# Two tiles for the squares of a layer normalisation, and one set of places for convolution inputs and feed-forward middle values

## The chip, the cores and the metric

The kernel runs as one program on 1 core of one Trainium2 chip. The metric is the device time of one execution in microseconds (us). Engine names: PE is TensorE's matmul, PEld its weight load, DVE is VectorE, ACT is ScalarE, POOL is GpSimd, SP is SyncE, which issues the DMAs of this kernel.

## The reference

The input is 4 images of 64 x 64 places with 96 channels. Each image goes through a chain of blocks:

```
x -> group norm -> 2-D selective scan (192 inner channels, 16 states, four scan directions) -> + x
  -> relu -> depthwise 3x3 convolution and pointwise product, batch norm            (layer1)
  -> + linear attention over the layer norm of the result                            (ln_a, attention)
  -> + feed-forward block over the layer norm of that, quantised to 8 bits           (q8, ffn2)
  -> + Fourier filter over the next layer norm                                       (ln_s, filter_*)
  -> + second quantised feed-forward block over a last layer norm                    (q8_3, ffn3)
```

The scan is h = exp(delta * A) * h + delta * u * B and y = sum over the states of h * C. A layer norm takes (x - mean) / sqrt(var + eps) over the 96 channels of a place. The feed-forward block rounds its operands to 8 bits and applies 96 -> 384 -> 96 channels with a relu between.

## The kernel before, in words

**The scans set the frame.** An image is held with channels on the partitions and 4096 places along them. The selective scan works on 192 phases (4 images, 2 orders of the places, 24 groups of 8 channels; 8 channels by 16 states fill 128 partitions). A phase has 4 chunks of 1024 places, gone through forwards and then backwards, so 8 steps. In a step ACT computes the decay exp(A * delta) into a PSUM tile `pa` (`decay`, L1495), DVE runs the scan (L1741 forwards, L1792 backwards) and adds the two directions (L1802), POOL multiplies by B and C (`times_b`, L1478, and `times_c`, L1482), PE sums over the states (`reduce`, L1509), ACT copies the sum (`result`, L1517), and SP loads and stores.

**Everything else is put beside the scans.** The other blocks are written as generators which yield a price per engine; after each step of a phase, `pieces` lets them advance as far as the step's credits go. This happens when the program is built: the order of instructions on each engine is fixed then, and every engine works through its own list in order. A side lane turns images for the second scan order and sums the scan's outputs; the main lane first prepares images 1 to 3 for their scans (`before_scans`), and then takes the rest of images 0, 1 and 2 (`rest`, with `deep` = 1), one after the other. The rest of image 3 comes after the last scan (`tail`, `deep` = 2). All beside the scans share 3 PSUM banks (`take` waits for a free one, and `give` hands it back).

**Around the change.** Each image has four layer norms (results `ln_a`, `q8`, `ln_s`, `q8_3`), each in two halves of 4 blocks of 512 places (`half_of`). For a block, PE subtracts the mean with one matmul into a PSUM bank (`p_mean`, L905). ACT copies it to SBUF (L894) and squares it into a tile `sq` (L897), both in `centred`, and then the bank is given back. PE averages the squares of the block into a part of the bank `p_var` (`variance`, L887). With `deep` = 1, the order inside a half is: mean matmul of block i, variance matmul of block i - 1, then the copy and square of block i. After four blocks, ACT, DVE and POOL form the reciprocal root (L926 to L937), PE spreads it (L957), and DVE scales (L948). With `deep` = 1 each half has one `sq` tile for its four squares; with `deep` = 2 it has four.

`layer1` reads its input in blocks of 8 rows plus a margin, into tiles `x` of 96 x 10 x 64 fp32 (2560 bytes in a partition) with two places (L820, loaded by L821), and 9 matmuls read each (L861). `feed_forward` holds the middle values of a block in `y16`, 128 x 3 x 512 fp16 (3072 bytes), two places as well (L1063, written by ACT at L785 and L794, read by POOL's cast to 8 bits at L1083). Both belong to the region `mid` of an image, in which layer1, three layer norms, the attention and the first feed-forward block are set up together. A pool gives each tag its own places; a tile that takes a place over waits for the work on the one that was there before.

Of the kernel before, what the change touches and what calls it, by code (L numbers as in the profile page):

```python
# [10 lines left out]
F32 = mybir.dt.float32  # L11
# [8 lines left out]
HW = 64  # L20
L = HW * HW
C = 96
# [4 lines left out]
BLK = 512  # L27
NBLK = L // BLK
RPB = BLK // HW
# [4 lines left out]
def conv_taps():  # L34

    return [(1, 1)] + [(y, x) for y in range(3) for x in range(3) if (y, x) != (1, 1)]


def tap_window(ky, kx, r0):

    dy, dx = ky - 1, kx - 1
    ra, rb = max(0, -dy - r0), min(RPB, HW - dy - r0)
    ca, cb = max(0, -dx), min(HW, HW - dx)
    return dy, dx, ra, rb, ca, cb
# [29 lines left out]
def layers(ctx: ExitStack, tc: tile.TileContext, a: dict, out):  # L74
# [48 lines left out]
    def steps_past(since, n):  # L123

        while ordered[0] and clock[0] < since + n:
            yield NEXT
# [53 lines left out]
    def rows_of(i):  # L180

        r0 = RPB * i
        return r0, max(r0 - 1, 0), min(r0 + RPB + 1, HW)
# [28 lines left out]
    def settle(held):  # L212


        while held:
            cost, f, args, since = held[0]
            if cost[1]:
                while ordered[0] and clock[0] == since and (clock[0] - 1) % 8 in (7, 0, 1):
                    yield NEXT
            yield cost  # L220
            held.pop(0)
            f(*args)

    def until(ready):
        while not ready():
            yield NEXT
# [549 lines left out]
    def blk(i):  # L776
        return slice(i * BLK, (i + 1) * BLK)
# [25 lines left out]
    def rest(b, take, deep, x1t=None, held=None):  # L803
# [9 lines left out]
        def layer1(wk):  # L813
            x3 = (x1[b] if x1t is None else x1t).rearrange("p (r w) -> p r w", w=HW)

            def load(i):
                r0, lo, hi = rows_of(i)
                if x1t is not None:
                    return x3[:, lo:hi, :], clock[0]
                x = wk.tile([C, RPB + 2, HW], F32, tag="x", name="x", bufs=2)  # L820
                nc.sync.dma_start(x[:, : hi - lo, :], x3[:, lo:hi, :])  # L821
                return x, clock[0]

            def arrived(i):
                return done.get(("x1", b), 0) >= min(i + 2, NBLK)

            yield from until(lambda: arrived(0))
            nxt = load(0)
            yield NEXT
            held = []  # L830

            def finish(i, p, give):
                nc.scalar.activation(
                    t[:, blk(i)], p, AF.Identity, scale=l1s[:, 0:1], bias=l1s[:, 1:2]
                )
                give()
                ready["t1"] = i + 1

            for i in range(NBLK):
                r0, lo, hi = rows_of(i)  # L840
                if nxt is None:
                    yield NEXT
                    yield from settle(held)
                    yield from until(lambda: arrived(i))
                    nxt = load(i)
                    yield NEXT
                (x, since), nxt = nxt, None
                if clock[0] < since + LANDING:
                    yield NEXT
                    yield from settle(held)  # L850
                    yield from steps_past(since, LANDING)
                p, give = yield from take("p_l1", C, held=held)
                p3 = p.rearrange("p (r w) -> p r w", w=HW)
                for k, (ky, kx) in enumerate(conv_taps()):
                    if k % 3 == 0:
                        yield (2.4, 0, 0, 0, 0 if k else 1)
                        if nxt is None and i + 1 < NBLK and arrived(i + 1):
                            nxt = load(i + 1)
                    dy, dx, ra, rb, ca_, cb_ = tap_window(ky, kx, r0)
                    at = r0 + dy - lo  # L860
                    nc.tensor.matmul(  # L861
                        p3[:, ra:rb, ca_:cb_], lhsT=taps[:, ky * 3 + kx, :],
                        rhs=x[:, at + ra : at + rb, ca_ + dx : cb_ + dx],
                        start=(k == 0), stop=(k == 8),
                    )
                    if k == 2:
                        yield from settle(held)
                held.append(((0, 0.68, 0, 0), finish, (i, p, give), clock[0]))
            yield NEXT
            yield from settle(held)  # L870

        def layernorm(wk, hold, dst, source, result, previous=None):
# [3 lines left out]
            def half_of(h):  # L876
# [6 lines left out]
                def variance():  # L883

                    i, sq = squares.pop(0)
                    at = 32 * (i - half[0])
                    nc.tensor.matmul(pv[at : at + 32, :], lhsT=mean_w, rhs=sq, start=True, stop=True)  # L887

                def centred(i, pm, give):
                    if squares and deep == 1:  # L890
                        variance()
                    sq = wk.tile([C, BLK], F32, tag=f"sq{h}", name="sq", bufs=1 if deep == 1 else 4)
                    if ordered[0]:
                        nc.scalar.copy(hold[:, blk(i)], pm)  # L894
                    else:
                        nc.vector.tensor_copy(hold[:, blk(i)], pm)
                    nc.scalar.activation(sq, pm, AF.Square)  # L897
                    give()
                    squares.append((i, sq))

                for i in half:
                    yield from until(lambda: count(source) > i)
                    pm, give = yield from take("p_mean", C, held=held)
                    yield (0.9, 0, 0, 0)
                    nc.tensor.matmul(pm, lhsT=centre, rhs=t[:, blk(i)], start=True, stop=True)  # L905
                    if squares and deep == 1:
                        yield (0.9, 0, 0, 0)
                        variance()
                    yield from settle(held)
                    held.append(((0, 1.25, 0, 0), centred, (i, pm, give), clock[0]))  # L910
# [415 lines left out]
        wk = normal.sbuf(f"ln{b}")  # L1326
# [8 lines left out]
        wk = mid.sbuf(f"mid{b}")  # L1335
# [24 lines left out]
        wk = last.sbuf(f"last{b}")  # L1360
# [287 lines left out]
    wk = weights.sbuf("weights", side="right")  # L1648
# [45 lines left out]
    wk = head.sbuf("pre0")  # L1694
# [14 lines left out]
    with tc.manual_schedule():  # L1709
        ordered[0] = True  # L1710
        pas = [decay(0, 0, True), None, None, None]
        for n in range(N + 1):
            h = n // NG
# [224 lines left out]
```

## Time and profile before

| | before |
|---|---|
| median of 3 runs | 5845.36 us (5842.83 to 5846.34) |
| profiled execution | 5842.19 us, span from first to last instruction 5840.4 us |
| busy: PE, DVE, ACT, POOL | 4230.1, 4797.6, 3044.6, 4416.6 us |
| mean granted TensorE clock | 0.775 of full speed |
| squares L897 in the scan part (images 0 to 2) | 96, median 592 ns, from 2029.1 to 5383.0 us |
| squares L897 in the tail (image 3) | 32 |
| ACT idle before the 96 squares | 75.2 us until p_var (43 times), 6.4 us until py (4 times) |
| a scan of 1024 places, L1741 | 2347 ns |
| a decay, L1495 | 1117 ns |

The busy time is the time in which an engine executes. The idle time listed with an instruction is the engine's time without work just before it; the name with it is the instruction that gave the last signal it waited for. An engine that is not the one on which the others wait in the end can idle at no cost. The first 520 us prepare image 0, from there to about 5440 us the scans run, and the last 400 us are the tail.

### The profile page before, as it was taken

Reading aid. Unit: us, or ns where it says so; the run is one execution under the profiler, and the core shown is the slowest. Engines: PE = TensorE matmul, PEld = TensorE weight load, DVE = VectorE, ACT = ScalarE, POOL = GpSimd, SP = SyncE. Lnnn points to the kernel's source line nnn. Section 1 sums busy time; section 2 is a strip of 40 time slices with the busy share of each in tenths; the row PEclk is TensorE's granted clock in tenths of the full one; section 3 lists DMA queues with packets and bytes.
Section 4 is the critical chain, followed back from the end, with each engine's and each line's share of the span. In section 5 each row is a group of like instructions: output and inputs, shape, how many; then the busy total and the mean of one; then the engine's idle time right before and its main releaser. Section 6 shows DMA issues by size and latency. Waiting matters only on the chain. (4 is left out here: it accounts for less than half of the span.)

```text
span 5840.4 us, 64640 instructions
## 1 busy us (share of the span) xinstructions
PE 4230.1 (72%) x19658; PEld 1612.3 (28%) x19658; DVE 4797.6 (82%) x3478; ACT 3044.6 (52%) x4205; POOL 4416.6 (76%) x2151
## 2 busy tenths in 40 slices
PE   8978888878973776664566776667678667667888
PEld 3322222222210221241331121245222114323345
DVE  2058898888899898998799999999999999979364
ACT  4667766766563346545454446444444554434233
POOL 1268888888889788888778989888898898867200
PEclk9979888888876776676777876668678767777888
DMA  3258878876698888788988867679887578886013
GB/s 105 80 163 233 234 215 225 242 221 195 187 253 237 222 216 223 206 243 237 246 240 224 228 185 211 194 212 249 230 235 206 164 210 235 245 230 191 22 39 104
DMA packets 469673, 1173.30 MB, mean 201 GB/s; under 512 B 90720, under 2 KB 155852, under 8 KB 469196
## 3 DMA queue, kind: packets, MB, share of 16 engines
q1 hardware_dynamic: 469324, 1169.17, 73.1%
q8 instruction: 156, 2.56, 0.2%
q14 instruction: 193, 1.58, 0.1%
HBM read 1012.05 MB, written 156.76 MB: 200 GB/s over the span
## 5 line engine op out<-in xcount | busy, mean ns | idle before, releaser
L1482 POOL TENSOR_TENSOR S<-S,rep 128x1024 f32<-128x1024 f32 x768 | 1807.6, 2356 | 541.5 <-DVE S L1802 485.4
L1495 ACT ACTIVATE pa<-dl,nega 128x1024 f32<-128x1024 f32 x1152 | 1285.3, 1117 | 1441.8 <-DVE S L1802 1076.0
L1478 POOL TENSOR_TENSOR B<-B,rep 128x1024 f32<-128x1024 f32 x768 | 1798.6, 2357 | 128.6 <-DMA B<-du_s 76.7
L1741 DVE TENSOR_TENSOR_SCAN S<-pa,S,B 128x1024 f32<-128x1024 f32 x576 | 1352.1, 2347 | 316.2 <-ACT pa L1495 128.6
L1509 PE MATMUL py<-S,red 128*32 128x512 f32 x3072 | 905.5, 845 | 739.9 <-POOL S L1482 491.4
L1792 DVE TENSOR_TENSOR_SCAN pa<-pa,edge,B 128x1024 f32<-128x1024 f32 x438 | 1029.7, 2351 | 46.3 <-ACT pa L1495 46.2
L1802 DVE TENSOR_TENSOR S<-S,pa 128x1024 f32<-128x1024 f32 x630 | 763.3, 1212 | 1.9
L1741 DVE TENSOR_TENSOR_SCAN S<-pa,B 128x1024 f32<-128x1024 f32 x192 | 436.4, 2273 | 189.5 <-ACT pa L1495 179.3
L390 PE MATMUL p_conv<-low,conv_w 128*96 128x512 f32 x1152 | 569.2, 647 | 8.7 <-ACT u L402 5.4
L1509 PEld LDWEIGHTS py<-S,red 128*32 128x32 f32 x3072 | 110.0, 125 | 1227.5 <-POOL S L1482 694.0
L1792 DVE TENSOR_TENSOR_SCAN pa<-pa,B 128x1024 f32<-128x1024 f32 x192 | 440.8, 2296 | 5.4
L154 ACT COPY side<-side 96x256 f32<-96x256 f32 (+1 forms) x448 | 278.9, 629 | 177.9 <-DMA deltaT_s<-side 74.5
L390 PE MATMUL p_conv<-high,conv_w 128*96 128x512 f32 (+1 forms) x768 | 356.6, 602 | 0.0
L1792 DVE TENSOR_TENSOR_SCAN dl<-pa,edge,B 128x1024 f32<-128x1024 f32 x138 | 323.1, 2341 | 16.3 <-ACT pa L1495 16.3
L1487 POOL TENSOR_TENSOR dl<-dl,rep 128x1024 f32<-128x1024 f32 x138 | 325.7, 2360 | 0.1
L1083 POOL CAST h<-y 128x1536 fp8e5<-128x1536 f16 x64 | 95.6, 1493 | 303.9 <-ACT y L794 286.3
L390 PEld LDWEIGHTS p_conv<-low,conv_w 128*96 128x96 f32 x1152 | 198.4, 179 | 390.8 <-issue 364.0
L905 PE MATMUL p_mean<-t,centre 96*96 96x512 f32 x256 | 174.8, 795 | 97.6 <-ACT sq L897 45.0
L1509 PE MATMUL py<-dl,red 128*32 128x512 f32 x552 | 219.2, 715 | 22.4 <-POOL dl L1487 22.3
L555 PE MATMUL p_y<-side,ident 96*96 96x512 f32 x336 | 207.1, 764 | 37.0 <-DVE q L948 11.6
L1517 ACT COPY ys<-py 128x512 f32<-128x512 f32 x384 | 221.9, 578 | 19.6 <-PE py L1509 18.2
L861 PE MATMUL p_l<-x,taps 96*96 96x504 f32 (+3 forms) x432 | 205.7, 629 | 16.4 <-DMA x<-x 12.5
(224 smaller groups left out, 5741.0 us busy)
## 6 DMA issues: line engine op xcount, KB each, us to landing
B<-du_s SPq DMA_DIRECT2D x768, 256.0 KB
dl<-delta_s SPq DMA_DIRECT2D x768, 256.0 KB
B<-duT_s SPq DMA_DIRECT2D x768, 256.0 KB
dl<-deltaT_s SPq DMA_DIRECT2D x768, 256.0 KB
z_s<-z SPq DMA_DIRECT2D x48, 512.0 KB
zl<-z_s SPq DMA_DIRECT2D x64, 384.0 KB
side<-y_s SPq DMA_DIRECT2D x120, 192.0 KB
rep<-bc_s SPq DMA_DIRECT2D x64, 256.0 KB
```

Source lines behind the costliest of these rows:

```text
L154: nc.scalar.copy(o.rearrange("p (w h) -> p w h", h=HW), t[:n, :].rearrange("p (h w) -> p w h", w=HW)[:, q * w : (q + 1) * w, :],)
L390: nc.tensor.matmul(p, lhsT=conv_w[: src.shape[0], k, oc * C : (oc + 1) * C], rhs=src[:, ky : ky + RPB, kx : kx + HW], start=(k == 0), stop ...
L555: nc.tensor.matmul(p, lhsT=ident[:C, :C], rhs=x, start=(j == 0), stop=(j == 2))
L1478: nc.gpsimd.tensor_tensor(Bs[n, q], Bs[n, q], reps[n // NG, 0, q], ALU.mult)
L1482: nc.gpsimd.tensor_tensor(Ss[n, q], Ss[n, q], reps[n // NG, 1, q], ALU.mult)
L1487: nc.gpsimd.tensor_tensor(dls[n, 0], dls[n, 0], reps[n // NG, 1, 0], ALU.mult)
L1495: nc.scalar.activation(pa, dls[n, q], AF.Exp, scale=nega[:, g : g + 1])
L1509: nc.tensor.matmul(py[32 * j : 32 * j + 32, :], lhsT=red, rhs=x[:, k * BLK : (k + 1) * BLK], start=(i == 0), stop=(i == len(terms) - 1),)
L1517: nc.scalar.copy(ys, pys.pop((n, half)))
L1741: nc.vector.tensor_tensor_scan(s, pas[q], Bs[n, q], Ss[n, q - 1][:, CH - 1 : CH] if q else 0.0, ALU.mult, ALU.add,)
L1792: nc.vector.tensor_tensor_scan(to[:, ::-1], pas[q][:, ::-1], Bs[n, q][:, ::-1], edge if k else 0.0, ALU.mult, ALU.add,)
L1802: nc.vector.tensor_tensor(Ss[n, q], Ss[n, q], to, ALU.add)
```

## The change

The convolution's input tile takes the tag `y16`, so that it shares the two places of the feed-forward block's middle values. The tile of the squares gets `2 * deep` places in each half: two instead of one beside the scans, four as before in the tail. In bytes of a partition of the region, 2 x 2560 go and 2 x 2048 come. An empty line moves the lines from 820 on by one in the changed kernel.

```diff
                 r0, lo, hi = rows_of(i)
                 if x1t is not None:
                     return x3[:, lo:hi, :], clock[0]
-                x = wk.tile([C, RPB + 2, HW], F32, tag="x", name="x", bufs=2)
+
+                x = wk.tile([C, RPB + 2, HW], F32, tag="y16", name="x", bufs=2)
                 nc.sync.dma_start(x[:, : hi - lo, :], x3[:, lo:hi, :])
                 return x, clock[0]
...
                 def centred(i, pm, give):
                     if squares and deep == 1:
                         variance()
-                    sq = wk.tile([C, BLK], F32, tag=f"sq{h}", name="sq", bufs=1 if deep == 1 else 4)
+                    sq = wk.tile([C, BLK], F32, tag=f"sq{h}", name="sq", bufs=2 * deep)
                     if ordered[0]:
                         nc.scalar.copy(hold[:, blk(i)], pm)
                     else:
                         nc.vector.tensor_copy(hold[:, blk(i)], pm)
                     nc.scalar.activation(sq, pm, AF.Square)
                     give()
                     squares.append((i, sq))
```

## The prediction

> **What bounds the kernel now.** The page first: busy time of each engine, then the costliest groups. Columns of a group: line, engine, operation, tiles and shapes, count | busy us, mean ns | idle of the engine just before it, and what ended it.
>
> ```profile
> PE 4230.1 (72%) x19658; PEld 1612.3 (28%) x19658; DVE 4797.6 (82%) x3478; ACT 3044.6 (52%) x4205; POOL 4416.6 (76%) x2151
> ...
> L1741 DVE TENSOR_TENSOR_SCAN S<-pa,S,B 128x1024 f32<-128x1024 f32 x576 | 1352.1, 2347 | 316.2 <-ACT pa L1495 128.6
> ...
> L1792 DVE TENSOR_TENSOR_SCAN pa<-pa,edge,B 128x1024 f32<-128x1024 f32 x438 | 1029.7, 2351 | 46.3 <-ACT pa L1495 46.2
> ```
>
> DVE is the busiest engine, and a scan waits most often for its decay tile, the exponential that ACT writes at L1495. The normalisation squares of images 0 to 2 lie between 2029 and 5383 us, so I asked for the stretch from 2000 to 5400 us (busy us and count of PE, PEld, DVE, ACT, POOL; granted PE clock; DMA share; GB/s):
>
> ```profile
> 2000.00:5400.00 3400.00, 2296.55 (x12618) 931.00 (x12618) 3100.90 (x2134) 1665.10 (x2269) 2862.38 (x1308) 0.73 0.81 220
> ```
>
> DVE is 91% busy there and idle for 299 us; POOL is next with 84%. So the time of this stretch is DVE's work plus its holes, and the wait that ends last in a hole decides. A faster ACT is worth only what it closes of these holes. Next, the line of the square, over the first 5500 us (who ended ACT's idle time before it, and who waited for it):
>
> ```profile
> L897 ACT ACTIVATE sq<-p_mean x96: 582/592/608, 2029.1 to 5383.0; 96x512 f32<-96x512 f32 x96
> ...
>   PE p_var L887: 75.2, 43
>   PE py L1509: 6.4, 4
> ...
>   PE p_mean L905: 45.0, 27
> ```
>
> ACT stands 81.6 us before 47 of the 96 squares, nearly all until PE has read the square before it. The timeline shows what that does (start, duration, engine, line, tiles, idle before and its releaser):
>
> ```profile
> 2029.71 2.02 PE L905 MATMUL p_mean<-t,centre 96*96 96x512 f32 x2 [2.09 <-ACT sq L897]
> ...
> 2031.66 1.91 PE L887 MATMUL p_var<-sq,mean_w 96*32 96x512 f32 x2
> 2031.77 0.58 ACT L894 COPY ln<-p_mean 96x512 f32<-96x512 f32 x1 [0.85 <-PE p_mean L905]
> ...
> 2033.67 0.59 ACT L897 ACTIVATE sq<-p_mean 96x512 f32<-96x512 f32 x1 [1.32 <-PE p_var L887]
> 2034.16 0.57 ACT L1517 COPY ys<-py 128x512 f32<-128x512 f32 x1
> ...
> 2034.63 1.12 ACT L1495 ACTIVATE pa<-dl,nega 128x1024 f32<-128x1024 f32 x1
> ...
> 2035.84 2.35 DVE L1741 TENSOR_TENSOR_SCAN S<-pa,S,B 128x1024 f32<-128x1024 f32 x1 [1.06 <-ACT pa L1495]
> ```
>
> The square holds ACT for 1.32 us after the copy, until the variance matmul of the previous square ends; a copy and the decay queue behind it, and the scan behind the decay starts 1.06 us late. PE's next mean matmul also waits for this square, because the square frees its PSUM bank.
>
> **What the skill says.** The Trainium skill, "Perfetto Trace Analysis", section "Per-engine timelines": an ACT instruction waits in its queue until all its semaphores are satisfied, and ACT and DVE are strict FIFO. The rows above agree: copy and decay run back to back once the square has gone. The same page, "Optimization Strategy", says to look for gaps on the most-contended engine and for the semaphore behind them, and that repeating gaps can mean too few buffers. The trace agrees for the square: its 47 holes average 1.74 us. No page prices this wait; all durations below are from the trace.
>
> **The change, part by part.** Order: the compiled instructions of PE, DVE, ACT, POOL and SP stand in the same order in both kernels, and nothing is added, removed or moved, no DMA either. Only waits differ.
>
> Part 1, convolution inputs in the feed-forward block's places: 24 loads at L821 keep two places and take turns as before. Each image's first use of a place by a middle value (L785) comes after all convolutions of that image, since it needs the second normalisation, which needs the whole attention. Cost nothing: those readers ended tens of us earlier. The tiles of this region lie elsewhere, which gives three ACT evacuations (L785, at 2486.43, 3764.67 and 4840.78) a later POOL instruction to wait for; in the trace it ends at 2440.13, 3718.45 and 4793.64, 46 us or more before it is needed. If that cover went, three waits would be at stake, some us each. The part alone: 0 us.
>
> Part 2, two squares a half: in each half's four squares (24 halves, 96 squares) the second loses its wait for PE, the third and fourth wait for a variance matmul one square older, on PE before the present mean matmul. In the sample that older matmul had ended 2 us or more before. The tail (image 3) had four tiles and keeps four, so its 32 squares do not change.
>
> What it is worth is not 81.6 us, since ACT is idle 51% of the stretch (1665 of 3400 busy). I went through the 47 waits, and took for each the DVE hole that the delayed decay causes, never more than the square's own wait. Starts of the scans and us: 2035.84 1.06; 2039.96 1.32; 2136.7 0.44; 2140.3 0.45; 2234.68 1.21; 2431.62 2.43; 3031 0.17; 3426.66 1.25; 3430.79 1.32; 3710.26 1.26; 4168.33 1.61; 4443.66 0.32; 4598.44 1.98; 4786.08 3.16; 5361 0.35. Sum 18.3. Behind the other waits the scans start without a hole that the decay causes.
>
> A second way goes over PE: the late square holds the PSUM bank, the attention product comes late, and DVE waits at L1037 with a scan queued behind. Waits of DVE between 3480 and 3512 us (total us, times, longest):
>
> ```profile
> DVE t L1037 <- PE p_att L1047: 4.7, 3, 2.3
> ```
>
> These three follow square waits of 3.01 and 2.50 us; with 0.28 and 1.47 us at 2212.42 and 2216.83, it is 6.45 us. At 4442.65 DVE waits 2.24 us for the rsqrt behind a square that itself waited 8.28 us (I take 1.8), and at 4595.77 1.06 us for p_rstd. Sum of this way 9.3. Both together: 27.6 us.
>
> What is late next: a scan that starts earlier meets its other feeders. After 2035.84 to 2039.96 the scan at 2062.48 starts only 0.09 us after a decay that waited 2.49 us for its DMA (issued at 2053.72 to 2054.89, behind other transfers on SP), so the 2.4 us won there can go again. With DMA busy 81% and POOL 84% of the stretch I keep three quarters: 21 us, and bounds of 0 (all given back) and 40 (half of the 81.6 reaches the end, because the halves also shorten PE's 45.0 us of waits at L905).
>
> Sum: profiled execution 5842.19 (span 5840.4, 1.8 around it) - 21 = 5821; the median of the three runs is 5845.36, 3.2 above the profiled one, so 5824.
>
> **Rivals.**
> A, the gain is given back: POOL and the transfers take the place of ACT as what ends the holes. For it: the scan at 2062.48, POOL at 84%, DMA at 81%. Against: of the DVE waits in the stretch 117 us end on the decay, while those that end on POOL or on the loads of B and dl are some 25 us together. It would leave about a quarter, 6 us: 5839.
> B, the gain is larger: PE's mean and variance chain runs without standing, everything beside the scans comes earlier, half of the 81.6 us counts: 5805. Against: ACT waits for DVE far longer (1076.0 us at L1495 behind L1802) than for PE here, so most of its time is free.
> C, slower: the same PE work in less time gets a lower clock. The clock is 0.73 in the stretch, against 0.81 between 560 and 1990 us[...]. A fall of 0.01 lengthens 2297 us of PE work by 31 us; DVE's waits that name PE are 59 of its 299 us of holes, so a fifth of that, 6 us, would reach the path. It decides against the change from a fall of 0.035 on; at 0.06 the time is 5845 + 36 - 21 = 5860. Against: nothing is added to PE, and 21 us of 3400 is 0.6% more load.
> D, no effect because the wait that went is not the last one: the copy before the square already waits for the mean matmul, 41.9 us in 23 waits. Against: in the rows above the square stands 1.32 us after the copy's end.
>
> **How the numbers follow.** Main case (half to all of 27.6 kept, 5818 to 5832) 0.62; A 0.19; B 0.08; C 0.07; D 0.04. About 0.2%, 12 us, is what a measurement tells from no change, so below 5833.7 counts as faster: the main case, B and a little of A (0.02), 0.72. A's rest and D are the same, 0.21. C is slower, 0.07. The range leaves out part of B and most of C: 5809 to 5845.
>
> **What would show it.** Right: at L897 the idle time until p_var falls from 75.2 us over the first 5500 us to below 25; DVE's waits for the decay between 2000 and 5400 us fall from 117 to about 100; DVE's share rises with the same busy time; everything before 2030 us and after 5440 us lasts as long as before. Wrong on giving back: the same fall at L897, but more waits of the scans for POOL or for loads. Wrong on the clock: less than 0.72 granted between 2000 and 5400 us. Wrong on part 1: any wait of L821 or L785 for POOL that was not there.

## The result and the profile after

| | before | changed |
|---|---|---|
| median | 5845.85 us (8 runs, 5840.30 to 5861.85) | 5826.24 us (8 runs, 5821.20 to 5830.70) |
| ratio | | 0.9965, 95% interval 0.9955 to 0.9975 |
| profiled execution, span | 5842.19, 5840.4 us | 5826.23, 5824.5 us |

The kernel became 19.6 us faster; the forecast was 5824 us with a range of 5809 to 5845. Measured once more beside other kernels, the ratio was 0.9951 (0.9934 to 0.9968). The page of the changed kernel, the lines that answer to those shown of before (lines from 820 on are one higher):

```profile
PE 4233.9 (73%) x19658; PEld 1615.2 (28%) x19658; DVE 4797.7 (82%) x3478; ACT 3044.1 (52%) x4205; POOL 4417.2 (76%) x2151
...
L1742 DVE TENSOR_TENSOR_SCAN S<-pa,S,B 128x1024 f32<-128x1024 f32 x576 | 1352.3, 2348 | 304.8 <-ACT pa L1496 108.5
...
L1793 DVE TENSOR_TENSOR_SCAN pa<-pa,edge,B 128x1024 f32<-128x1024 f32 x438 | 1029.8, 2351 | 46.8 <-ACT pa L1496 46.6
```

No engine works less: the busy times are those of before within 4 us. What went is idle time. Ahead of the first group of scans it fell by 11.4 us, from 316.2 to 304.8: the part that ended on the decay fell by 20.1 (128.6 to 108.5), and other waits of the same group grew by 8.7. The stretch from 2000 to 5400 us, and the line of the square over the first 5500 us (two of its 98 rows are the tail's):

```profile
2000.00:5400.00 3400.00, 2309.34 (x12644) 937.96 (x12642) 3114.54 (x2146) 1669.78 (x2275) 2874.97 (x1315) 0.73 0.82 221
```

```profile
L898 ACT ACTIVATE sq<-p_mean x98: 581/595/616, 2034.3 to 5500.0; 96x512 f32<-96x512 f32 x98
...
  PE p_var L888: 7.2, 8
...
  PE py L1510: 1.0, 1
...
  PE p_mean L906: 43.2, 19
```

The square's wait until PE has read the square before it fell from 75.2 to 7.2 us; with the waits until py, 47 holes of 81.6 us became 9 of 8.2. DVE does 13.6 us more of its unchanged work in the same 3400 us. The granted clock is 0.73 as before. The last line shows what hardly changed: PE's mean matmul still stands 43.2 us for a square (45.0 before), because the square gives its PSUM bank back; the experiments on the bank come to that.

The timeline of the changed kernel at the place that the prediction showed (start, duration, engine, line, tiles, idle before and its releaser):

```profile
2034.89 1.10 PE L906 MATMUL p_mean<-t,centre 96*96 96x512 f32 x2 [2.09 <-ACT sq L898]
...
2035.92 1.04 PE L888 MATMUL p_var<-sq,mean_w 96*32 96x512 f32 x2
2036.04 0.57 ACT L895 COPY ln<-p_mean 96x512 f32<-96x512 f32 x1
2036.52 0.59 ACT L898 ACTIVATE sq<-p_mean 96x512 f32<-96x512 f32 x1
2037.00 0.58 ACT L1518 COPY ys<-py 128x512 f32<-128x512 f32 x1
...
2037.46 1.13 ACT L1496 ACTIVATE pa<-dl,nega 128x1024 f32<-128x1024 f32 x1
...
2040.15 2.35 DVE L1742 TENSOR_TENSOR_SCAN S<-pa,S,B 128x1024 f32<-128x1024 f32 x1 [0.19 <-DMA yT_s<-ys]
```

The square now follows its copy at once, while PE is still at the variance matmul of the square before it; copy and decay follow. The scan behind this decay, which stood 1.06 us before, stands 0.19 us, and for a transfer. The order of the instructions is unchanged. One thing differs that the tiles do not explain: the mean matmul takes 1.10 us here and took 2.02 us before. That comes back below.

### The profile page after: what moved, and what is told of

It is laid out like the page before. It is cut to its first block, busy times and chain, and to the rows that moved or that the text cites. A ratio compares the mean times of both kernels' runs of the same rounds, so it can differ in the third digit from the quotient of the medians.

```text
span 5824.5 us, 64622 instructions
## 1 busy us (share of the span) xinstructions
PE 4233.9 (73%) x19658; PEld 1615.2 (28%) x19658; DVE 4797.7 (82%) x3478; ACT 3044.1 (52%) x4205; POOL 4417.2 (76%) x2151
## 5 line engine op out<-in xcount | busy, mean ns | idle before, releaser
L1742 DVE TENSOR_TENSOR_SCAN S<-pa,S,B 128x1024 f32<-128x1024 f32 x576 | 1352.3, 2348 | 304.8 <-ACT pa L1496 108.5
L1793 DVE TENSOR_TENSOR_SCAN dl<-pa,edge,B 128x1024 f32<-128x1024 f32 x138 | 323.1, 2341 | 15.5 <-ACT pa L1496 15.2
L906 PE MATMUL p_mean<-t,centre 96*96 96x512 f32 x256 | 175.7, 800 | 97.8 <-ACT sq L898 43.2
L862 PE MATMUL p_l<-x,taps 96*96 96x504 f32 (+3 forms) x432 | 200.9, 616 | 15.0 <-DMA x<-x 13.6
```

Source lines behind the costliest of these rows:

```text
L1742: nc.vector.tensor_tensor_scan(s, pas[q], Bs[n, q], Ss[n, q - 1][:, CH - 1 : CH] if q else 0.0, ALU.mult, ALU.add,)
L1793: nc.vector.tensor_tensor_scan(to[:, ::-1], pas[q][:, ::-1], Bs[n, q][:, ::-1], edge if k else 0.0, ALU.mult, ALU.add,)
```

## The experiments

All ratios are to the kernel before, measured on the same chip in the same row of runs.

**Each part alone.** Part 1: only the first edit.

```diff
-                x = wk.tile([C, RPB + 2, HW], F32, tag="x", name="x", bufs=2)
+                x = wk.tile([C, RPB + 2, HW], F32, tag="y16", name="x", bufs=2)
```

> Part 1 alone: the convolution inputs share the places of the feed-forward block's middle values, and each half keeps its one tile for squares. The forecast's own theory (the waits of the squares carry the gain): 0 us, a ratio of 1.000 within 0.0015, and ACT's idle time before the 96 squares until p_var stays at 75 us (65 to 85). Rival (the shared places, or where the tiles then lie, carry part of the gain): a ratio of 0.9985 or less, with waits of ACT, POOL or SP that become shorter at L821, L785 or L1083.

Measured: 0.9997 (0.9985 to 1.0009), and 75.9 us of waits for p_var before the squares. By itself the sharing is not told apart from nothing. It is meant for room: the second tile of each half adds 2 x 2048 bytes of a partition, and the sharing frees 2 x 2560. No run shows whether the tiles would fit without it.

Part 2 alone, in a form that needs no room:

```diff
-                    sq = wk.tile([C, BLK], F32, tag=f"sq{h}", name="sq", bufs=1 if deep == 1 else 4)
+                    sq = wk.tile([C, BLK], F32, tag="sq" if deep == 1 else f"sq{h}", name="sq", bufs=2 * deep)
```

> Part 2 alone, in another way: the two halves of a normalisation take turns on the two tiles for squares that they had one each of, so that a half has two, no byte is added, and the convolution inputs keep their own places. The squares theory: as the changed kernel, a ratio of 0.9965 (0.995 to 0.998), idle before the squares until p_var below 15 us. Rival (the sharing carries part): clearly less than the changed kernel, 0.998 or more.

Measured: 0.9947 (0.9926 to 0.9968) with 9.6 us left of the wait for p_var. The ratio lies just below the expected 0.995 to 0.998, so there is more gain than expected. Its interval covers the changed kernel's 0.9965, but both ran once more in one row:

> The changed kernel once more, beside the next three on the same chip: ratio to the kernel before 0.9965 (0.9955 to 0.9975). It gives the measure for the others of this row.

> The halves that take turns on two tiles, a second time, since the first measurement (0.9947, 0.9926 to 0.9968, of four executions) overlaps with the changed kernel's but lies lower. The squares theory: no difference to the changed kernel, 0.9965 within 0.001. Rival (the sharing of places costs some 10 us in the changed kernel, which the sharing alone did not show): 0.9947 again, and 0.0015 or more below the changed kernel of this row.

Measured: the changed kernel 0.9951 (0.9934 to 0.9968), the halves that take turns 0.9944 (0.9925 to 0.9963). The changed kernel's ratio lies a little below its expected range this time, so its gain is 20 to 24 us by the medians of the two rows. The two kernels of this row differ by 0.0007, less than the 0.0015 that the rival asked for and less than either interval. The squares make the gain, with or without the shared places; that the sharing costs a few us stays possible within these intervals.

**Is it the square's wait, or the time of ACT's pair?** One tile, PE's order changed:

```diff
+                    if squares and deep == 1:
+                        yield (0.9, 0, 0, 0)
+                        variance()
                     yield (0.9, 0, 0, 0)
                     nc.tensor.matmul(pm, lhsT=centre, rhs=t[:, blk(i)], start=True, stop=True)
-                    if squares and deep == 1:
-                        yield (0.9, 0, 0, 0)
-                        variance()
```

> One tile for squares as before, but PE does the variance matmul of the previous square ahead of the mean matmul of this block instead of after it, so that the square finds its tile free when the mean is there; nothing else is moved. Theory that the time of ACT's pair (copy and square) counts, whoever it waits for: the idle time before L897 until p_var falls below 10 us, but the mean matmul comes one variance matmul (1 to 2 us) later, the copy's wait for p_mean grows by 30 us or more, and most of the gain is lost: ratio 0.999 to 1.002. Rival (the square's wait as such is what costs, whatever takes it away): 0.9965 like the changed kernel.

Measured: 1.0009 (0.9999 to 1.0018). ACT's idle time before the copy (first fence) and before the square (second), first 5500 us:

```profile
  PE p_mean L908: 71.7, 39
```

```profile
  PE p_var L887: 57.5, 29
```

The square's wait did not fall below 10 us as expected, but only from 81.6 to 57.5: the last square of a half, whose predecessor's variance matmul stands outside the edited loop, still waits, 36.9 us of the 57.5 (31.7 before). The copy's wait rose from 41.9 to 71.7 us, as expected. So 24 us less wait before the square bought nothing: the copy ahead of it waited 30 us more. This fits the first theory, that the sum before the pair counts: 123.5 us before, 129.2 here, and 57.1 in the changed kernel, where no matmul is put later. The rival, 0.9965, is out.

**The bank.** One tile, the bank given back after the copy:

```diff
                         nc.scalar.copy(hold[:, blk(i)], pm)
+                        give()
+                        nc.scalar.activation(sq, hold[:, blk(i)], AF.Square)
                     else:
                         nc.vector.tensor_copy(hold[:, blk(i)], pm)
-                    nc.scalar.activation(sq, pm, AF.Square)
-                    give()
+                        nc.scalar.activation(sq, pm, AF.Square)
+                        give()
```

> One tile for squares as before, but the square reads the copy in SBUF instead of the PSUM bank, and the bank is given back after the copy, so that PE no longer waits for a late square to get a bank; ACT still waits for p_var before the square. If the second way (late bank, late attention product, 9.3 us in the forecast's sum) works through the bank: 7 us faster, ratio 0.9988 (0.998 to 0.9995), and DVE's waits for p_att at L1037 between 3480 and 3512 us fall from 4.7 to under 2.5 us. If the bank is not what counts: 1.000, with PE's wait for p_var's own square unchanged. In both cases the scans' holes behind the decay stay, since ACT's wait stays.

Measured: 0.9984 (0.9976 to 0.9993). That is as expected of a bank that counts, and 1.000 lies outside the interval: giving the bank back early gains with one tile too. The square itself became longer, 630 ns from SBUF against 592 from PSUM, and its wait shorter, 64.4 us with the part until py:

```profile
  PE p_var L887: 60.0, 36
```

The copy's wait for the mean fell as well, from 41.9 to 32.7 us. So the early bank also shortens the queue before copy and square, and the run doesn't separate the two ways of the forecast. The waits for p_att between 3480 and 3512 us were gone in this trace, but that is no evidence, as the part on the clock shows. The same edit on top of the changed kernel:

> The changed kernel, and the square reads the copy in SBUF, so that the bank goes back after the copy, some 0.5 us before the square's end in each of 96 blocks. In the changed kernel PE still stands 43 us at L906 for a square. If PE's wait for the bank still has a part on the path: 3 to 6 us below the changed kernel, 0.9955 to 0.9960, PE's waits at L906 for the square gone and for the copy about 35 us instead. If two tiles have taken all there was on this way: same as the changed kernel within 0.0005.

Measured: 0.9943 (0.9923 to 0.9964), against 0.9951 (0.9934 to 0.9968) of the changed kernel in the row. PE's waits for the square were gone and 33.5 us until the copy stood in their place, as expected; but the 3 us between the medians are inside the intervals, so what that is worth stays open.

**Is there more to be had?** Four tiles in one set (`tag="sq"`, `bufs=4` beside the scans), alone and with the bank's edit:

> The changed kernel with its four tiles for squares as one set for both halves, so that a half has four and no square waits for PE; no byte more. The changed kernel's rest of 8 us of waits at L898 goes to 0. The squares theory: of 8 us at most a third was on the path, so 0 to 3 us below the changed kernel: 0.9960 to 0.9966. Rival B of the forecast (more than the holes counted there is to be had from the chain of mean and variance matmuls): 0.9950 or less.

> Four tiles in one set for both halves, and the bank given back after the copy: both rests of the changed kernel taken away. If what is left of the squares' waits (8 us) and of PE's waits for the bank (43 us) is off the path: as the changed kernel, 0.9945 to 0.9965. If their small parts add: 0.9935 or less.

Measured: 0.9948 (0.9931 to 0.9965) and 0.9949 (0.9937 to 0.9961). No square waits for PE in either. Four tiles alone fall below the 0.9950 set for rival B, but the changed kernel itself measured 0.9951 beside them, so this border tells nothing. Neither version is told apart from the changed kernel (the second ran in another row, without it), and none is shown to beat it. Rival B's 40 us would be a ratio of 0.9932. That is outside both intervals of the changed kernel, though inside some of the wider ones of its relatives.

**Do the places add up?** Two tiles, shared by both halves, only in some normalisations (the other squares keep one tile a half; the second kernel has "q8" and "q8_3" instead). The edit is to the changed kernel, without its old line:

```diff
+                    twice = deep == 1 and result in ("ln_a", "ln_s")
+                    sq = wk.tile(
+                        [C, BLK], F32, tag="sqd" if twice else f"sq{h}", name="sq",
+                        bufs=2 if twice else 1 if deep == 1 else 4,
+                    )
```

> Two tiles for squares only in the normalisations ahead of the attention and of the Fourier filter (results ln_a and ln_s); the two ahead of the feed-forward blocks (q8 and q8_3) keep one. By the forecast's list these sites hold 14.8 of its 27.6 us; two of them (2.4 us, at 2036 and 2040 us) were holes of one execution's low clock, so 12.4, of which three quarters reach the end: 9 us, ratio 0.9984 (0.9975 to 0.9993). Idle before the squares until p_var falls to about half. Rival (one stretch gives all of it, or nothing adds up): below 0.997, or 1.000.

> The complement: two tiles only in the normalisations ahead of the feed-forward blocks (q8 and q8_3). The forecast's list holds 12.8 us there, 6.5 of them through the attention product; three quarters are 10 us: ratio 0.9983 (0.9975 to 0.9993), and together with the other half the 20 to 28 us of the changed kernel. DVE's waits for p_att at L1037 between 3470 and 3520 us go from 4.7 to below 2.5 us here and stay near 4.7 us in the other half. Rival as there.

Measured: 0.9966 (0.9952 to 0.9979) for ln_a and ln_s, 0.9981 (0.9971 to 0.9991) for q8 and q8_3. The second is as expected. The first is 20 us and not 9: its interval overlaps the expected one, but the ratio misses it and lies below the 0.997 set for the rival that one stretch gives all. That rival fails all the same, since the second kernel gains too, with 1.000 outside its interval. The two gains add up to 0.53%, which agrees with the 0.35% and 0.49% of the whole within the intervals. The waits before the squares were 53.3 and 35.5 us, so the kernel with more waits left had the larger gain by the medians; the intervals overlap. The sites in the traces, below, tell the two apart better.

**The clock.** The attention product was to show the second way, by DVE's waits for p_att. With two tiles only in ln_a and ln_s they were to stay near 4.7 us, and the trace has none there; in the kernel with two tiles and the early bank they are back, between 3480 and 3520 us:

```profile
DVE t L1040 <- PE p_att L1050: 4.1, 3, 1.9
```

What tells these executions apart is the clock granted to PE. First the kernel with two tiles and the early bank at that place, then the kernel before, then the changed kernel (busy us and count of PE, PEld, DVE, ACT, POOL; clock; DMA share; GB/s):

```profile
3494.00:3504.00 10.00, 10.00 (x15) 1.84 (x14) 6.14 (x5) 3.92 (x6) 8.62 (x4) 0.55 0.85 211
```

```profile
3494.00:3507.00 13.00, 11.18 (x14) 1.93 (x15) 9.11 (x7) 6.52 (x9) 13.00 (x6) 0.50 0.74 215
```

```profile
3490.00:3503.00 13.00, 11.70 (x36) 2.50 (x36) 12.97 (x12) 8.71 (x12) 11.76 (x7) 1.00 0.92 226
```

At half clock DVE has its holes there; at full clock it has none. One tile or two makes no difference to that. (Only the doubled matmuls, below, have 1.8 us there at full clock.) Part 1 alone, with one tile, also met half clock there (0.50 from 3502 to 3514 us) and has the holes (first). The kernel with two tiles only in ln_a and ln_s, so with one at this place, met full clock and has none (second):

```profile
DVE t L1037 <- PE p_att L1047: 4.8, 3, 2.3
```

```profile
3490.00:3503.00 13.00, 9.17 (x27) 1.78 (x26) 12.96 (x10) 8.70 (x12) 11.76 (x6) 1.00 0.85 231
```

The same holds for the place of the timeline, before (first) and with part 1 alone (second), both with one tile:

```profile
2030.00:2034.00 4.00, 3.57 (x4) 0.29 (x3) 4.00 (x3) 1.83 (x3) 4.00 (x2) 0.50 1.00 204
```

```profile
2036.00:2040.00 4.00, 3.26 (x11) 0.64 (x10) 3.89 (x3) 3.33 (x7) 4.00 (x3) 1.00 0.86 212
```

With part 1 alone the square there waits 0.45 us instead of 1.32, and the scan behind it has no hole that the decay causes. So those two sites of the forecast's list (2.4 us) and the three at p_att (4.7 us) were holes of the clock that the execution happened to have there, and their closing in the changed kernel's trace is not shown to be the tiles' doing.

**More of the wait.** One tile, each variance matmul done twice beside the scans:

```diff
-                    nc.tensor.matmul(pv[at : at + 32, :], lhsT=mean_w, rhs=sq, start=True, stop=True)
+                    for _ in range(2 if ordered[0] else 1):
+                        nc.tensor.matmul(pv[at : at + 32, :], lhsT=mean_w, rhs=sq, start=True, stop=True)
```

> One tile for squares as before, and PE does each of the 96 variance matmuls beside the scans twice in a row (the second writes the same sums again), so that the wait of the next square gets longer by one such matmul, 1.0 us at the full PE clock and some 2 us at half of it. ACT's idle time before the 96 squares should grow from 82 us by 60 to 90 us. The changed kernel took 74 us of it away and became about 20 to 24 us shorter, so 0.28 to 0.33 of a us of this wait reaches the end: 17 to 30 us longer, ratio 1.003 to 1.005. Rival (PE's chain itself is the bound, the wait only shows it): all 96 doubled matmuls, some 130 us, appear in good part, ratio 1.010 or more. Rival (only single sites at low clock matter): no change, 1.000 to 1.001.

Measured: 1.0089 (1.0072 to 1.0105), 52 us by the ratio and 50 between the medians, more than the theory. The first rival's border, 1.010, lies inside the interval. Before the squares stand 130.5 us:

```profile
  PE p_var L888: 125.0, 50
  PE py L1510: 5.5, 4
```

That is 49 us more, less than the expected 60 to 90, and the end moved by about as much. It is not the price of the wait alone: the added matmuls also delay what PE does next. DVE's waits for p_rstd grew from 34.6 us (2000 to 5400 us) to 54.8 (2000 to 5450 us in this longer kernel), those for the decay from 117.3 to 140.4. The expectation was missed. The variance matmuls alone are busy 99 us more, and about half of that reaches the end; the run gives no coefficient for the tile.

**The forecast's sites in all traces.** Ten entries of the forecast's list, from 2234.68 to 5361 us (without 3031, and with the 1.8 us of the second way at 4443), come to 16.7 us. For each I took the time from the start of the scan before to the start of this scan, and how much shorter it was than in the trace of before:

| traces | ten sites together, us shorter |
|---|---|
| changed kernel, twice | 16.6, 17.3 |
| halves that take turns, twice | 17.1, 16.7 |
| four tiles; two tiles and early bank; four tiles and early bank | 18.3; 18.2; 18.6 |
| two tiles in ln_a and ln_s only | 10.5 |
| two tiles in q8 and q8_3 only | 6.4 |
| one tile: part 1 alone; PE's order; early bank | 2.8; -1.7; 3.9 |
| one tile, variance matmuls doubled | -15.7 |

Taken together, the holes at these sites are closed by the tiles: all seven traces with more than one tile in every normalisation have them, none with one tile has more than 3.9 us. Doubling the variance matmul makes the same intervals longer. They follow the tile site by site: 2431.62, 3426.66, 3430.79 and 4786.08 (7.6 us) close in the ln_a and ln_s kernel and not in the other, while 2234.68, 4598.44 and 5361 (4.3 us), and most of 4168.33, close in the q8 and q8_3 kernel and not in the first. Two sites are less sure: 3710.26 and 4443.66 also get shorter in traces with one tile. At 2035.84 and 2039.96 the interval is shorter by 0.9 and by 1.0 to 1.5 us in every trace but that of before, whatever the tiles, which is again the clock of one execution.

## Why the prediction was right, point by point

- **Total**: 21 us forecast, 19.6 measured, 24 between the medians of the second row. The direction and the range hold. The first way, the queue behind the square, is shown by the tiles alone (0.9947 and 0.9944) and by the sites. Of the second way it is shown that an early bank gains (0.9984); that it does so through the attention product is not shown, since the holes counted there were the clock's.
- **Part 1 at nothing**: 0.9997. No wait at L821 or L785 for POOL came with part 1 alone. In the changed kernel's trace one of 1.7 us stands at L785, for POOL's writing of a tile of the attention (`lt`). By the prediction's own sign that counts against part 1, but the same wait (1.7 and 1.0 us) is in both traces of the halves that take turns, which do not share the places, so it comes with the tiles for squares.
- **Idle time at the square**: below 25 us forecast, 7.2 measured. By place in the half, with the waits until py, the second, third and fourth square waited 20.5, 29.4 and 31.7 us before, and 0, 2.9 and 5.3 in the changed kernel. That is the pattern that the prediction's part 2 describes.
- **Waits for the decay** in the stretch: 117 to about 100 forecast, 98.4 measured (78.2, 15.2 and 5.0). This sign proves little by itself: part 1 alone, with one tile, has 103.5 there and no gain, and the halves that take turns, with two, 88.8 and 107.6.
- **The list of sites**: ten entries, 16.7 us forecast, came to 16.6 to 18.6 in the traces with more tiles; eight of them follow the tiles alone. The sites at 2036 and 2040 us and the ones at p_att, 7.1 us of the 27.6, belong to the clock. Taking one execution's holes as the kernel's was a step of the working that I did not mark as uncertain, and it was wrong for a quarter of the list.
- **"I keep three quarters"**: luck in part. The quarter was withheld for giving back, 6.9 us; the holes that were never the kernel's are 7.1 us, so the sum came out near 21 for a reason other than the one given. What was really given back can't be told: the later rows gained 24 to 29 us. Away from the sites the step from one scan to the next differs by up to 3.1 us between two executions, in both directions.
- **"Everything before 2030 us lasts as long"**: missed in the trace. The first square starts 5.2 us later in the changed kernel's, and 5.1 us later with part 1 alone. Over all fourteen traces it starts between 2023.2 and 2035.4 us, with one tile and with two, so it is the spread of single executions. The part after the last scan's start is as before, 451.1 and 449.5 us.
- **Rival A** (given back to POOL and loads): the scans' waits for POOL's B went from 7.3 to 10.3 us, those for the loads of B from 11.1 to 10.6, and the quarter of the gain that A would leave, 6 us, is outside the result. But something of the kind is in the trace: DVE's waits for transfers of every kind grew from 50.8 to 63.0 us in the stretch. The traces with one tile lie between 50.8 and 65.1, those with more in every normalisation between 59.8 and 79.4, so how much of it is the change's stays open.
- **C** (lower clock): 0.73 in both. Its premise, more load and less clock, has no support in the two stretches that it compared: PE was busy 68% where the clock was 0.73, and 77% where it was 0.81.
- **D** (not the last wait): the halves that take turns refute it. The reordered matmuls fit what was right in it: the copy's wait for the mean counts too.
- **Open**: how the gain divides between the queue and the bank, and what a us of this wait is worth; the doubled matmuls mix it with PE's own delay.

## What to carry to other kernels

A wait on an engine that is half idle is worth the holes it makes on the busiest engine, and a list of these holes, each capped by the wait itself, gave the size here for the sites that were the kernel's. Take the wait away without delaying what comes before it: the reordered matmuls removed 30% of the wait and gained nothing, the second buffer removed nine tenths and gained 0.35 to 0.5%. And a hole in one trace may belong to that execution, as a quarter of this list did: read the granted clock at the place before counting it, and look at the same place in a second trace of a kernel in which it should not have changed.

## What the runs showed of the hardware

The clock granted to PE is 0.5 or 1.0 and nothing between in the trace of the kernel before from 2000 to 5400 us, in some 310 stretches, and where a stretch lies differs from one execution to the next of instructions in the same order. In all fourteen traces every stretch lasts a whole multiple of 3.41 us. A mean matmul took 1.10 us at full and 2.02 at half clock. The Trainium skill, "TensorE: Matmul & The Clock Gate", section "Part 1: The HAM clock gate (the "warmup" mystery)", says that the gate has these two states, follows how busy PE has been, and works in free-running windows, so that the same kernel differs from run to run. The two values and the difference agree. That a busy PE gets the full clock does not hold here, as far as the profile's busy time tells, in which the ends of matmuls are modelled: PE was busy in all of 10.00 us at 0.55. What decides the clock of a busy PE stays open.
